# Two-layer network on one core: where the first layer's sums, statistics and comparisons stand in VectorE's queue

## The chip, the cores and the metric

The kernel runs on one core of one Trainium2 chip. A core has five engines with queues of their own: TensorE (PE; its weight loads are listed as PEld), VectorE (DVE), ScalarE (ACT), GpSimd (POOL) and SyncE (SP), which here only issues DMAs. Each engine works through its own queue in the order in which the program was written, and semaphores make one engine wait for another. The metric is the time of one execution in device microseconds, a median over runs.

## What is computed

A batch of 8 sequences of 512 tokens with 512 features goes through two layers. The first is a graph attention, the second a self-attention with conditioned normalization. Cut to what matters:

```
# layer 0: graph attention over the first 20 tokens, for d = 0, 1 (labels, labels transposed)
row_zero  = v.sum(-1) == 0
q_exp     = where(row_zero[..., None], 0, q[:, None, :])
self_feat = concat([v, q_exp], -1) @ W_self.T + b_self
kv        = self_feat[:, :20]
qh, kh    = self_feat @ Wq.T + bq,  kv @ Wk.T + bk          # 16 heads of 32
A         = labels[:, :, :20, :]                            # 11 labels an edge, 0 or 1
mask      = A.sum(-1) > 0
aff       = where(mask, qh.kh / sqrt(32), -9e15) + (A @ w_bias + b_bias)
out_d     = (softmax(aff) @ kv) @ Wout + bout
x         = v + relu(self_feat + out_0 + out_1)
# layer 1
h   = norm(x) * gamma(cond) + beta(cond)
att = softmax(q k^T) v / sqrt(512),  q, k, v from h
h1  = att @ Wp.T + bp + x
out = norm(h1) * gamma(cond) + beta(cond) + h1
```

All of it is fp32.

## The kernel before

**Stages.** A prologue (to about 77 us) prepares weights and the keys of the first layer. Then come 32 *slots* of the first layer (to about 391 us), one for each batch b = 0 to 7 and block c = 0 to 3 of 128 tokens, numbered n = 4b + c. The second layer follows, 128 steps in an order of its own, and is not touched.

**The order is written by hand.** The slots run under a manual schedule: each engine gets its instructions in the order in which the loop at L627 calls the helpers, so a line that moves in the loop moves in the queue of every engine that it uses.

**A slot's scores** pass through five engines, three slots long. In slot n, `scores0` (L525) makes the scores of slot n + 2: TensorE multiplies into a pair of PSUM banks (L532), VectorE adds a row and brings them to SBUF (L536), GpSimd multiplies by the mask (L538). `add_edges` (L541) adds the label bias on GpSimd (L542). `less_top` (L545) takes the maxima on VectorE (L549) and subtracts them on GpSimd (L550). In slot n + 1, `normalize0` (L552) takes exponentials on ScalarE (L553), sums and reciprocals on VectorE (L556, L557), and multiplies on GpSimd (L558). In slot n + 2, `turn_weights` turns the weights on TensorE (L564) and ScalarE copies them out (L566); `result0` (L569) multiplies them with the values (`po`, L574, L576), VectorE adds to the input (L577), and SP stores the block.

**The edges' masks and biases** are made two blocks ahead by `edges` (L248) on VectorE: half 0 sums the 11 labels (L258) and compares with zero (L259), half 1 multiplies by the weights (L262), sums (L263) and adds the constant (L264). For the last block of a batch `far_away` (L266) folds the mask into the bias (L269, L270).

**self_feat of a later batch** comes out of seven quarter products (L347; numbers 1, 2 at c = 2, 6, 7 at c = 3, 4, 5 at c = 0, 3 at c = 1), with sums of weights and of turned tokens made beforehand (`turned_sums` on GpSimd, L345). Each product goes from PSUM into a quarter of `SF` (L373). Three sums of products (`Y0`: product 1, 1 + 6, 1 + 6 + 7) go into four quarters; these adds are gathered in `TO_ADD0` and made at the slot's end (L698 to L700): one at c = 2, three at c = 3.

**Live tokens** are those whose features do not sum to zero. `live_sums` (L289) makes four copies with an accumulated sum on ScalarE (L293) and a comparison on VectorE (L295); `live_of` (L297) turns the result to a row on TensorE (L301) and copies it (L303), for use at c = 2 (L366). For batch b + 2 the sums stand at the end of c = 0 and the row in c = 1 ahead of `result0`.

**The second layer's start** lies in the last slots: statistics of the first finished batch (`norm_stats`, L93, L95, L96 on VectorE, a power on GpSimd, L97) at n = 15 to 18, and its normalization (`norm`, L111 on VectorE) at n = 22 and 23, two blocks each.

Most PSUM banks come from a ring of four (`bank`), score and weight pairs from a ring of two (`pair`).

Of the kernel before, what the change touches and what calls it, by code (L numbers as in the profile page):

```python
# [9 lines left out]
F32 = mybir.dt.float32  # L10
# [3 lines left out]
ALU = mybir.AluOpType  # L14
# [4 lines left out]
B, N, F = 8, 512, 512  # L19
P = 128  # L20
# [5 lines left out]
D2 = 2 * NG  # L26
HM = H * D2
KB = HM // P
L = 11
# [15 lines left out]
def graph_then_self_attention(ctx: ExitStack, tc: tile.TileContext, x, x_t, near, near_t, labels, w_self_t, wq, wk_t,  # L45
                              wout_t, wg_t, wb_t, wqkv_t, wp_t, cols, gate_vecs, rows, out):
    nc = tc.nc
# [13 lines left out]
    edge_bc = vec[:, nv + C * DH:]  # L61
# [28 lines left out]
    def statistics(src, name):  # L90

        st = small.tile([P, 6], F32, tag="st", name=f"st_{name}")
        nc.vector.bn_stats(st, src)  # L93
        mv = small.tile([P, 2], F32, tag="mv", name=f"mv_{name}")
        nc.vector.bn_aggr(mv, st)  # L95
        nc.vector.tensor_scalar(mv[:, 1:2], mv[:, 1:2], EPS, None, ALU.add)  # L96
        nc.gpsimd.tensor_tensor(mv[:, 1:2], mv[:, 1:2], minus_half[:, 0:1], ALU.pow)  # L97
        STATS[name] = mv
# [5 lines left out]
    def norm_stats(b, c, src=None):  # L104
        statistics((src or XQ[b])[:, c, :], f"{b}_{c}")
# [68 lines left out]
    with ExitStack() as l0:  # L174
# [3 lines left out]
        pro = l0.enter_context(tc.tile_pool(name="pro", bufs=1))  # L178
# [36 lines left out]
        def load_vt(b):  # L215
            VT[b] = turned.tile([P, C, N], F32, tag="turned", name=f"vt_{b}")
            for cut in (slice(0, 2), slice(2, C)) if b == 0 else (slice(0, C),):
                nc.sync.dma_start(VT[b][:, cut], blocks(x_t[b])[:, cut])
# [20 lines left out]
            nc.vector.memset(head[DH * j:DH * (j + 1), j:j + 1], 1.0)  # L239

        MASK, ADD, LABELS = {}, {}, {}

        def load_labels(b, halves=(0, 1)):
            for i in halves:
# [3 lines left out]
        def edges(b, c, halves=(0, 1)):  # L248


            if c == 0 and 0 in halves:
                MASK[b] = two.tile([P, C, D2], F32, tag="mask", name=f"mask_{b}")
                ADD[b] = two.tile([P, C, D2], F32, tag="add", name=f"add_{b}")
            src = LABELS[b, c // 2][:, c % 2, :].rearrange("p (m l) -> p m l", l=L)
            weighted = src.bitcast(F32)
            total = two.tile([P, D2], F32, tag="total", name=f"total_{b}_{c}_{halves[0]}")
            if 0 in halves:
                nc.vector.tensor_reduce(total, src, AX.X, ALU.add)  # L258
                nc.vector.tensor_scalar(MASK[b][:, c, :], total, 0.0, None, ALU.is_gt)  # L259
            if 1 not in halves:  # L260
                return
            nc.vector.tensor_tensor(weighted, src, edge_bc[:, None, 0:L].to_broadcast([P, D2, L]), ALU.mult)  # L262
            nc.vector.tensor_reduce(total, weighted, AX.X, ALU.add)  # L263
            nc.vector.tensor_scalar(ADD[b][:, c, :], total, edge_bc[:, L:L + 1], None, ALU.add)  # L264

        def far_away(b):  # L266

# [21 lines left out]
        def live_sums(b):  # L289

            sums = two.tile([P, C], F32, tag="sums", name=f"sums_{b}")
            for c in range(C):
                nc.scalar.activation(X[b][:, c, :], X[b][:, c, :], AF.Copy, accum_out=sums[:, c:c + 1])  # L293
            LT[b] = two.tile([P, C], F32, tag="lt", name=f"lt_{b}")
            nc.vector.tensor_scalar(LT[b], sums, 0.0, None, ALU.not_equal)  # L295

        def live_of(b):  # L297

            pl = bank(f"pl_{b}") if b else pair("pl_0")[:, 0, :]
            for c in range(C):  # L300
                nc.tensor.transpose(pl[:, c * P:(c + 1) * P], LT[b][:, c:c + 1].to_broadcast([P, P]), ident)  # L301
            LIVE[b] = two.tile([P, N], F32, tag="live", name=f"live_{b}")
            nc.scalar.copy(LIVE[b], pl)  # L303
# [25 lines left out]
        SA, TB, Y0, TO_ADD0 = {}, {}, {}, []  # L329
# [100 lines left out]
        for c in range(C):  # L430
            edges(0, c)
# [109 lines left out]
        def add_edges(b, c, engine=nc.gpsimd):  # L541
            engine.tensor_tensor(T[b, c], T[b, c], ADD[b][:, c, None].to_broadcast([P, H, D2]), ALU.add)  # L542
# [26 lines left out]
        def result0(b, c):  # L569
            cut = slice(c * P, (c + 1) * P)  # L570
            po = bank(f"po_{b}_{c}")

            for g in range(HG):
                nc.tensor.matmul(po[:, g * P:(g + 1) * P], SF[b][:, g, cut], ident, is_transpose=True, start=(g == 0), stop=False)  # L574
            for i in range(KB):
                nc.tensor.matmul(po[:, 96 * i:96 * i + P], WT[b, c][:, i, :], vo[:, b % 2, i, :], start=False, stop=(i == KB - 1))  # L576
            nc.vector.scalar_tensor_tensor(X[b][:, c, :], po, 0.0, X[b][:, c, :], ALU.max, ALU.add)  # L577
            nc.sync.dma_start(mid[b, c * P:(c + 1) * P, :], X[b][:, c, :])
# [48 lines left out]
        for n, (b, c) in enumerate(slots):  # L627
            turn_weights(b, c)

            if n + 3 == len(slots):  # L630
                scores0(*slots[n + 2])
            if n + 1 < len(slots):
                normalize0(*slots[n + 1])
            if n + 3 < len(slots):
                scores0(*slots[n + 2])
            if n + 2 < len(slots):
                add_edges(*slots[n + 2], nc.vector if n + 3 == len(slots) else nc.gpsimd)
            if n < 2:
                self_feat(1, (c + 2,))
            elif b + 1 + c // 2 < B:  # L640
                for i in ((4, 5), (3,), (1, 2), (6, 7))[c]:
                    self_feat_product(b + 1 + c // 2, i)
            if 26 <= n < len(slots) - 2:
                less_top(*slots[n + 2])
            if c == 1 and b + 2 < B:
                live_of(b + 2)
                if b + 3 < B:
                    load_vt(b + 3)
            if n in (10, 11, 12, 13):
                keys(1, n - 10, 0)  # L650
            if n in (24, 25):
                for f in (2 * (n - 24), 2 * (n - 24) + 1):
                    turn(0, f)
            group = {26: lambda: q_or_k(0, 0), 27: lambda: q_or_k(1, 0), 29: lambda: value(0), 30: lambda: value(1),
                     31: lambda: value(2)}.get(n, lambda: None)()
            if group:
                group.half(0)
                if n < 30:
                    group.half(1)
            if n == 10:  # L660
                gate_columns(gb)
            result0(b, c)
            if n >= 30:
                group.half(1)
            if b + 1 + c // 2 < B:
                edges(b + 1 + c // 2, (c + 2) % 4, (0,))
            if n < 26:
                less_top(*slots[n + 2])
            if n in (10, 11, 12, 13):
                keys(1, n - 10, 1)  # L670
            if b + 1 + c // 2 < B:
                edges(b + 1 + c // 2, (c + 2) % 4, (1,))
            if c == 0 and b + 2 < B:
                live_sums(b + 2)
            if c == 1:
                if b + 1 < B:
                    far_away(b + 1)
                    load_vo(b + 1)
                if b + 2 < B:
                    load_labels(b + 2, (1,))  # L680
            if c == 0 and b + 2 < B:
                load_labels(b + 2, (0,))
            if c == 2 and b + 2 < B:
                q_row(b + 2)
            if c == C - 1 and b + 3 < B:
                load_x(b + 3)
            if n == 4:
                WG = [weight("wg", wg_t), weight("wb", wb_t)]
            if n == 8:
                gb = gate_vectors()  # L690
                WQ.update({(d, 1): weight(f"wq{d}_1", wq[d]) for d in range(2)})

            if n < 2:
                for i in ((0, 1), (3, 2))[n]:
                    weight_sums0(i)
            if b + 2 + c // 3 < B:
                turned_sums(b + 2 + c // 3, (0, 1, 3, 2)[c])
            for sf, y in TO_ADD0:  # L698
                nc.vector.tensor_tensor(sf, y, sf, ALU.add)
            TO_ADD0.clear()  # L700

            if n in (17, 18, 19, 24):
                i = min(n - 17, 3)
                W1.append(weight(f"w1_{i}", (*(wqkv_t[i] for i in range(3)), wp_t)[i]))
            if n in (23, 28):
                fetch((n - 23) // 5)
            if n == 9:
                early = weight("early", mid[0])
            if 15 <= n < 19:
                norm_stats(0, n - 15, early)  # L710
            for i in {22: (0, 1), 23: (2, 3)}.get(n, ()):
                norm(0, i, early)


# [332 lines left out]
    with tc.manual_schedule():  # L1047
# [22 lines left out]
        for n, (b, g, c) in enumerate(steps):  # L1070
# [28 lines left out]
            early = n % 2 == 0 or each  # L1099
# [12 lines left out]
            if at in OUTPUT_SUMS_AT:  # L1112
                back, i = OUTPUT_SUMS_AT[at]
# [94 lines left out]
```

## Time and profile before

| | us |
|---|---|
| median of 3 runs | 1317.75 (1315.42 to 1318.74) |
| the profiled execution | 1315.49 |
| its span, first to last instruction | 1313.7 |
| granted TensorE clock in it | 0.999 |

The profile is one execution on the chip. Busy time is counted by engine; idle time before an instruction is given with the instruction or semaphore that ended it (its releaser). A line such as L556 is a line of the kernel. A group written "out<-in" tells which tile is written and which are read. Rows that matter for the change, with count, busy time and the mean of one, all on VectorE unless said otherwise:

| line | what | count | busy us | mean ns |
|---|---|---|---|---|
| L259 | mask, 128x40 | 32 | 19.3 | 604 |
| L264 | constant of the bias, 128x40 | 32 | 14.5 | 453 |
| L699 | gathered adds, 128x512 | 24 | 19.7 | 857 |
| L549 | maxima, 128x640 to 128x32 | 32 | 26.2 | 819 |
| L556 | sums of exponentials | 32 | 26.0 | 813 |
| L293 | sums of live tokens (ScalarE) | 32 | 19.8 | 623 |
| L345 | sums of turned tokens (GpSimd), the 12 plain ones | 12 | 19.0 | 1585 |
| L558 | normalized weights (GpSimd) | 32 | 40.7 | 1273 |

### The profile page before, as it was taken

Reading aid. Unit: us, or ns where it says so; the run is one execution under the profiler, and the core shown is the slowest. Engines: PE = TensorE matmul, PEld = TensorE weight load, DVE = VectorE, ACT = ScalarE, POOL = GpSimd, SP = SyncE. Lnnn points to the kernel's source line nnn. Section 1 sums busy time; section 2 is a strip of 40 time slices with the busy share of each in tenths; the row PEclk is TensorE's granted clock in tenths of the full one; section 3 lists DMA queues with packets and bytes.
Section 4 is the critical chain, followed back from the end, with each engine's and each line's share of the span. In section 5 each row is a group of like instructions: output and inputs, shape, how many; then the busy total and the mean of one; then the engine's idle time right before and its main releaser. Section 6 shows DMA issues by size and latency. Waiting matters only on the chain.

```text
span 1313.7 us, 29713 instructions
## 1 busy us (share of the span) xinstructions
PE 1295.4 (99%) x11347; PEld 988.2 (75%) x11347; DVE 974.7 (74%) x1775; ACT 710.1 (54%) x1740; POOL 842.1 (64%) x905
## 2 busy tenths in 40 slices
PE   9999999999999999999999999999999999999997
PEld 6568887777765687777777777777777777777775
DVE  4479887888746678587677859767775976776886
ACT  2333233223225566766666676675666666666664
POOL 0067775677653546677578667747856775775776
PEclk9999999999999999999999999999999999999999
DMA  9533553253221000001002000100200010010010
GB/s 344 180 108 115 179 194 104 96 180 95 92 80 57 1 1 2 2 17 66 1 1 81 1 2 17 66 2 2 81 2 1 18 66 1 2 50 1 10 42 33
DMA packets 46491, 78.65 MB, mean 60 GB/s; under 512 B 9680, under 2 KB 14224, under 8 KB 46352
## 3 DMA queue, kind: packets, MB, share of 16 engines
q1 hardware_dynamic: 45920, 76.22, 17.0%
q8 instruction: 91, 1.49, 0.5%
q10 hardware_dynamic: 432, 0.55, 0.1%
q14 instruction: 48, 0.39, 0.1%
HBM read 59.27 MB, written 17.49 MB: 58 GB/s over the span
## 4 chain that ended last, share of the span: by engine, by line
PE 87%; DVE 8%; POOL 2%; issue 1%; ACT 1%; DMA 0%; POOLq 0%; DVEq 0%; ACTq 0%
PE pst L793 19%; PE pt L949 17%; PE s L924 10%; PE pss L532 8%; PE pao L964 8%; PE psp L836 6%; PE psf_p L359 4%; PE psf L312 2%; PE po L576 2%; PE pqk L138 2%; DVE top L931 2%; PE pz L124 1%; PE ptw L564 1%; PE pw L501 1%; PE pq L482 1%
## 5 line engine op out<-in xcount | busy, mean ns | idle before, releaser
L944 POOL TENSOR_SCALAR e<-e,den 128x512 f32<-128x512 f32 x511 | 366.8, 718 | 262.4 <-DVE den L941 168.5
L936 ACT ACTIVATE e<-s,top 128x512 f32<-128x512 f32 x512 | 348.9, 699 | 131.4 <-DVE top L931 131.2
L931 DVE TENSOR_REDUCE top<-s 128x2 f32<-128x1024 f32 x256 | 301.2, 1218 | 18.5 <-PE s L924 17.1
L949 PEld LDWEIGHTS pt<-ident,e 128*128 128x128 f32 x2048 | 234.5, 141 | 82.5 <-POOL e L944 25.9
L949 PE MATMUL pt<-ident,e 128*128 128x128 f32 x2048 | 289.7, 276 | 3.4 <-ACT et L951 1.3
L951 ACT COPY et<-pt 128x512 f32<-128x512 f32 x369 | 209.6, 597 | 101.1 <-PE pt L949 100.5
L924 PE MATMUL s<-k_pair,q_pair 32*128 32x512 f32 x992 | 143.8, 640 | 0.0
L532 PE MATMUL pss<-kq,sf 128*128 128x320 f32 x512 | 142.9, 432 | 0.0
L964 PEld LDWEIGHTS pao<-et,v 128*32 128x32 f32 x4096 | 107.5, 110 | 44.4 <-issue 44.4
L964 PE MATMUL pao<-et,v 128*32 128x128 f32 x4096 | 126.5, 274 | 0.0
L532 PEld LDWEIGHTS pss<-kq,sf 128*128 128x128 f32 x512 | 94.9, 190 | 36.1 <-ACT kq L489 0.3
L936 ACT ACTIVATION_READ_ACCUMULATOR e<-s,top 128x1 f32 x512 | 109.4, 214 | 0.0
L951 DVE COPY et<-pt 128x512 f32<-128x512 f32 x143 | 96.4, 674 | 3.4 <-PE pt L949 2.8
L538 POOL TENSOR_TENSOR t<-t,mask 128x640 f32<-128x640 f32 x32 | 49.5, 1547 | 65.6 <-DVE t L536 65.6
L558 POOL TENSOR_TENSOR t<-t,den 128x640 f32<-128x640 f32 x32 | 40.7, 1273 | 54.9 <-DVE den L557 54.3
L553 ACT ACTIVATE t<-t 128x640 f32<-128x640 f32 x32 | 23.6, 738 | 91.5 <-POOL t L550 91.5
L550 POOL TENSOR_TENSOR t<-t,top 128x640 f32<-128x640 f32 x32 | 47.4, 1480 | 38.9 <-DVE top L549 38.9
L126 ACT ACTIVATE ht<-pz,gates_t 128x512 f32<-128x512 f32 x32 | 24.7, 778 | 64.2 <-PE pz L124 64.2
L924 PEld LDWEIGHTS s<-k_pair,q_pair 32*128 32x128 f32 x992 | 41.2, 182 | 20.8 <-issue 17.4
L566 ACT COPY wt<-ptw 128x640 f32<-128x640 f32 x32 | 22.2, 694 | 61.2 <-PE ptw L564 61.1
L851 DVE TENSOR_TENSOR xq<-psp,xq 128x512 f32<-128x512 f32 x30 | 20.2, 689 | 45.9 <-PE psp L836 40.7
L793 PE MATMUL pst<-t,w 128*128 128x256 f32 x224 | 53.7, 383 | 0.0
(272 smaller groups left out, 2286.4 us busy)
## 6 DMA issues: line engine op xcount, KB each, us to landing
x<-in_x SPq DMA_DIRECT2D x8, 1024.0 KB
mid<-x SPq DMA_DIRECT2D x32, 256.0 KB
xq<-mid SPq DMA_DIRECT2D x8, 1024.0 KB
out<-o SPq DMA_DIRECT2D x31, 256.0 KB
vt<-in_x_t SPq DMA_DIRECT2D x7, 1024.0 KB
labels<-in_labels SPq DMA_DIRECT2D x16, 440.0 KB
wq<-in_wq SPq DMA_DIRECT2D x4, 1024.0 KB
gate<-gates SPq DMA_DIRECT2D x8, 512.0 KB
```

What stands on the lines that cost most here:

```text
L359: nc.tensor.matmul(o[:, m, :], a[:, k, m * P:(m + 1) * P], t[:, k, :], start=(k == 0), stop=(k == 1))
L532: nc.tensor.matmul(o, SF[b][:, k, cut], KQ[b][:, k, on], start=(k == 0), stop=(k == C - 1))
L538: nc.gpsimd.tensor_tensor(t, t, MASK[b][:, c, None].to_broadcast([P, H, D2]), ALU.mult)
L793: nc.tensor.matmul(out[:, m, :], fixed[:, k, m * P:(m + 1) * P], moving[:, k, :], start=(k == 0), stop=(k == 1))
L836: nc.tensor.matmul(out[:, m, :], t[:, k, m * P:(m + 1) * P], a[:, k, :], start=(k == 0), stop=(k == 1))
L924: nc.tensor.matmul(S[n][j // 2][:, j % 2, :], Q[b, g][on, c * P:(c + 1) * P], K[b, g][on, :], start=True, stop=True)
L931: nc.vector.tensor_reduce(TOP[n][:, 2 * pair:2 * pair + 2], S[n][pair], AX.X, ALU.max, negate=True)
L936: nc.scalar.activation(e, S[n][pair][:, j % 2, :], AF.Exp, bias=TOP[n][:, j:j + 1], accum_out=DEN[n][:, j:j + 1])
L944: engine.tensor_scalar(E[n][j], E[n][j], DEN[n][:, j:j + 1], att_scale, ALU.mult, ALU.mult)
L949: nc.tensor.transpose(pt[:, k * P:(k + 1) * P], E[n][j][:, k * P:(k + 1) * P], ident)
L951: copy(et, pt.rearrange("p (k n) -> p k n", k=C))
L964: nc.tensor.matmul(PAO[b, g][DH * j:DH * (j + 1), at], V[b][:, k, DH * h:DH * (h + 1)], ET[n, j][:, k, :], start=(k == 0), stop=(k == C - 1))
```

## The change

Five things, all in the first layer:

- The gathered adds: instead of all that are on the list, each slot makes one, the oldest. The three of c = 3 are so spread over c = 3, c = 0 and c = 1.
- The statistics of n = 15 to 18 stand between the two halves of `edges`, ahead of the maxima, instead of at the slot's end. Block 0 and 1 of the normalization are made at n = 21 and 22, blocks 2 and 3 at n = 23 as before.
- The sums of live tokens go from the end of c = 0 to c = 1, behind the scores of that slot; the comparison L295 on VectorE goes with them.
- The row of live tokens goes behind `result0` in c = 1, on TensorE and ScalarE.
- The two comparisons and additions with a scalar in `edges` become operations on two tensors, the second one a column repeated along the row; a column of zeros is set once for it.

The count of instructions stays on TensorE, ScalarE, GpSimd and SP, and the order of SP's queue too; VectorE has one memset more.

```diff
         MASK, ADD, LABELS = {}, {}, {}
+        nothing = pro.tile([P, 1], F32, name="nothing")
+        nc.vector.memset(nothing, 0.0)
...
                 nc.vector.tensor_reduce(total, src, AX.X, ALU.add)
-                nc.vector.tensor_scalar(MASK[b][:, c, :], total, 0.0, None, ALU.is_gt)
+                nc.vector.tensor_tensor(MASK[b][:, c, :], total, nothing.to_broadcast([P, D2]), ALU.is_gt)
...
             nc.vector.tensor_reduce(total, weighted, AX.X, ALU.add)
-            nc.vector.tensor_scalar(ADD[b][:, c, :], total, edge_bc[:, L:L + 1], None, ALU.add)
+            nc.vector.tensor_tensor(ADD[b][:, c, :], total, edge_bc[:, L:L + 1].to_broadcast([P, D2]), ALU.add)
...
                 add_edges(*slots[n + 2], nc.vector if n + 3 == len(slots) else nc.gpsimd)
+            if c == 1 and b + 2 < B:
+                live_sums(b + 2)
             if n < 2:
                 self_feat(1, (c + 2,))
...
-            if c == 1 and b + 2 < B:
-                live_of(b + 2)
-                if b + 3 < B:
-                    load_vt(b + 3)
+            if c == 1 and b + 3 < B:
+                load_vt(b + 3)
...
             result0(b, c)
+            if c == 1 and b + 2 < B:
+                live_of(b + 2)
             if n >= 30:
                 group.half(1)
             if b + 1 + c // 2 < B:
                 edges(b + 1 + c // 2, (c + 2) % 4, (0,))
+            if 15 <= n < 19:
+                norm_stats(0, n - 15, early)
             if n < 26:
                 less_top(*slots[n + 2])
             if n in (10, 11, 12, 13):
                 keys(1, n - 10, 1)
             if b + 1 + c // 2 < B:
                 edges(b + 1 + c // 2, (c + 2) % 4, (1,))
-            if c == 0 and b + 2 < B:
-                live_sums(b + 2)
...
-            for sf, y in TO_ADD0:
+            if TO_ADD0:
+                sf, y = TO_ADD0.pop(0)
                 nc.vector.tensor_tensor(sf, y, sf, ALU.add)
-            TO_ADD0.clear()
...
-            if 15 <= n < 19:
-                norm_stats(0, n - 15, early)
-            for i in {22: (0, 1), 23: (2, 3)}.get(n, ()):
+            for i in {21: (0,), 22: (1,), 23: (2, 3)}.get(n, ()):
                 norm(0, i, early)
```

## The prediction

> **What bounds the kernel now.** I read the page's first part, then the busy time by stretch (prologue, the 32 slots of the first layer, the second layer), then what TensorE itself waited for, then the chain and the timeline around those waits. Columns of the stretch: us, then busy time and instructions of PE, PEld, DVE, ACT, POOL, then clock and DMA. Of a wait: total us, times, longest.
>
> ```profile
> PE 1295.4 (99%) x11347; PEld 988.2 (75%) x11347; DVE 974.7 (74%) x1775; ACT 710.1 (54%) x1740; POOL 842.1 (64%) x905
> ...
> 76.60:391.00 314.40, 307.77 (x1816) 243.35 (x1815) 257.72 (x468) 96.95 (x189) 213.74 (x149) 1.00 0.37 122
> ...
> PE ptw L564 <- POOL t L558: 3.5, 7, 1.0
> PE pq L482 <- DVE x L577: 1.6, 4, 0.4
> PE po L574 <- DVE sf L373: 1.4, 1, 1.4
> ```
>
> TensorE is the bound; only where it idles is there time to win. In the slots it idles 314.4 - 307.8 = 6.6 us. The change moves work of VectorE, ScalarE and GpSimd in the slots, and only four transposes a batch on TensorE, so what it can win is small.
>
> A slot starts at its first L564 matmul. Undisturbed slots last 9.86 us (slots 2, 3) and, for c=1, 8.63 (slot 9); slot 24, with two turns of 0.44 more, would last 10.73. Against these the slots lose, idle and refill together: slots 4 to 6: 0.30, 0.44, 0.06; 16 to 19: 0.66, 0.65, 0.81, 0.06; 20 to 22: 1.12, 0.43, 0.06; 23: 0.56; 24: 1.72. Sum 6.9. The L482 waits (slots 10 to 13) are for a PSUM bank that L577 reads out; this edit leaves them.
>
> The timeline at the largest L564 wait (slot 20; start, us, engine, line, then idle and its releaser):
>
> ```profile
> 293.14 2.96 DVE L699 TENSOR_TENSOR sf<-ys,sf 128x512 f32<-128x512 f32 x3
> 293.14 1.80 POOL L345 TENSOR_TENSOR ts<-vt 128x512 f32<-128x512 f32 x1
> 293.21 0.74 ACT L553 ACTIVATE t<-t 128x640 f32<-128x640 f32 x1 [4.01 <-POOL t L550]
> 296.02 0.81 DVE L556 TENSOR_REDUCE den<-t 128x32 f32<-128x640 f32 x1
> ...
> 297.36 1.27 POOL L558 TENSOR_TENSOR t<-t,den 128x640 f32<-128x640 f32 x1 [2.41 <-DVE den L557]
> ...
> 298.69 0.77 PE L564 MATMUL ptw<-ident,t 128*128 128x128 f32 x5 [0.95 <-POOL t L558]
> ```
>
> The exponentials are there at 293.95, but L556 starts at 296.02: three adds stand before it. The second took 1.75 us where 0.68 is usual: it waits for L345 to end on GpSimd. The same triple stands ahead of slots 4, 16 and 24.
>
> **One add a slot.** The 24 adds stay; two of each triple move to the ends of the next two slots. Slot 20: one add issues in 0.60, and L556 follows the exponentials, 2.05 earlier; these also come some 0.6 sooner (293.35), since slot 18's statistics (below) fall into 1.6 us in which L549 waited for L542, and VectorE enters slot 19 in time. L558 then ends near 296.0, and TensorE wants it at 287.71 + 9.86 = 297.57: the stall goes (-1.12). What is late next is L577, which must now wait for `po` (297.8; it was 299.66). L558's earlier end also starts L538 and L542 earlier (L542 to 299.4), so the maxima end at 300.3 and the exponentials for slot 22 at 302.7, against 305.04. The add moved to this slot stands ahead of L556, where the trace has 0.69 us of idle time waiting for the exponentials; it costs nothing. Slot 21's loss (0.43) goes. In slot 21 L542 ends 2.25 earlier (308.57, was 310.82), the slot itself 1.55. The third add follows L270, which waits for L345 anyway, and with one L111 (below) puts 0.60 + 0.54 ahead of L556: L558 ends 316.2, where TensorE wants it at 316.06. 0.1 is lost, and 0.6 more if that earliness is not there. Slots 20 to 22: **-1.5**.
>
> Slots 4 to 6, likewise: L556 moves from 123.93 to 121.90, L577 is back at `po` (126.5, was 127.58), **-0.8**. Slots 23 and 24: L111's first (1.49 us in slot 22, waiting for L345) stays, its second (0.54) goes to slot 21, where GpSimd should be idle: slot 23 -0.3. In slot 24 L574 waits 1.44 for L373, which reads out the bank that `po` takes. VectorE comes to slot 24 earlier by what TensorE gains before it, and two adds less put L373 another 1.20 ahead; with less idle time to refill after, 1.3 of the 1.72 goes. Together **-1.6**.
>
> **Statistics ahead of the maxima** (slots 15 to 18). L93, L95, L96 issue in 0.60 + 0.22 + 0.18 = 1.0 us and now stand before L549 instead of before L556. Where VectorE is late the total is the same; where L556 waits for exponentials, 1.0 is put into the chain L549, L550 (1.58), L553 (0.74). The power on GpSimd (L97, 0.55) goes ahead of L550, but beneath L549 (0.82). Slot 15 pays out of its two removed adds: L556 at 253.1 instead of 255.17, slot 16's 0.66 goes. In slot 16 L549 begins at 259.87 (was 260.95), exponentials end at 263.1. In slot 17 the statistics follow a mask that waits for L542 until 269.0; L549 at 269.9 (was 270.22), and the third add ahead of L556 leaves L558 ending 277.0 (was 277.74): slot 18 keeps its stall. Slots 16 to 19: **-0.7**.
>
> **Comparisons.** Every L259 and L264 stays one instruction. Uncontended rows: 184 and 245 ns. The nearest tensor_tensor is L270, 128x160 in 326 ns; 120 fewer elements at 1/0.96 ns give 201 (the clock from "VectorE: DVE Perf Modes" of the Trainium skill, an estimate). So +17 and -44 ns. The bounds are wide, though: the same L259 takes 0.18 us or 1.3.
>
> ```profile
> 87.88 0.18 DVE L259 TENSOR_SCALAR mask<-total 128x40 f32<-128x40 f32 x1
> ...
> 101.37 1.28 DVE L270 TENSOR_TENSOR add<-add,far 128x160 f32<-128x160 f32 x1
> ...
> 289.14 1.54 POOL L542 TENSOR_TENSOR t<-t,add 128x640 f32<-128x640 f32 x1
> 289.41 1.30 DVE L259 TENSOR_SCALAR mask<-total 128x40 f32<-128x40 f32 x1
> 290.71 0.82 DVE L549 TENSOR_REDUCE top<-t 128x32 f32<-128x640 f32 x1
> ```
>
> The held L259 ends 35 ns after L542: it waits for GpSimd. If a tensor_tensor didn't, all 32 masks would give back 19.3 - 32 x 0.184 = 13.4 us and the 32 sums 14.5 - 7.8 = 6.7. But L270, a tensor_tensor of two SBUF operands, waits too (1.28 for 0.33). The Trainium skill ("SBUF — State Buffer", Who interferes with whom) speaks against this edit in the same way: a Vector instruction with two SBUF inputs contends with a GpSimd instruction that reads SBUF. By row and rule the waits stay: 0. No row has an operand repeated along its innermost dimension, as `nothing` is; that is the open point. And even unheld, L549 reads what L542 writes and would wait just as long; only the statistics of slots 16 to 18 could use the hole, at most 0.9 each, -1.2 of the stalls left. I take **0**, bounds 0 and -1.2; the 32 masks' +17 ns hide in those same waits. The added memset lies under the prologue's DMA waits.
>
> **Sums and row of live tokens.** The four activations and readouts (L293, 2.54 us) go from the end of c=0 to behind the exponentials of c=1; L295 goes behind L536, L301 behind `po`, L303 behind it on ScalarE. The queue of SP keeps its order (vt's load issues as before). ScalarE has room: 2.3 to 3 of 9 us in slots 5, 17, 21. New waits: VectorE's L295 for the sums, with L373 and L577 queued behind it, and TensorE's L301 for L295, with the next L564 queued behind. TensorE comes to L301 8.63 - 0.44 = 8.19 after a slot's start; L295 is ready 2.54 + 0.2 after the exponentials. So it is free if these end by 5.4. In the trace they end at 4.8 (slot 1), 4.6 (9), 6.35 (5), 6.36 (17), 6.35 (21); with the adds gone I get 4.8 for slot 5 (131.15 - 126.3), 5.1 for 21 (302.7 - 297.57), 5.9 for 17 (263.1 - 257.18): 0.6 lost in slot 17, counted in its -0.7. In slot 13 L301 fills the 0.4 wait for L577, but L303 then holds a bank for L482: 0.
>
> **Sum**: 0.8 + 0.7 + 1.5 + 1.6 = 4.6 of the 6.9. The profiled execution took 1315.49 (span 1313.7 and 1.8 around it): 1310.9. The median shown is 1317.75, 2.3 above it; the same 4.6 off gives **1313.1**.
>
> **Rivals.**
> 1. A repeated operand leaves GpSimd alone. For it: no row tests it. Against: rule and L270. Then -4.6 - 1.2 = -5.8: about 1312.0, to 1310.9 if all 6.9 goes.
> 2. The lateness moves instead of going. An add put at the end of c=0 meets L345, and if GpSimd starts first costs 1.75, not 0.68 (in the trace VectorE started first in each slot where one add stood there); the third add has no cover to spare. With 1.1 in three of these slots, 3.3 of the gain goes back: -1.3, near 1316.5. For it: GpSimd is 64% busy and every hold is passed on.
> 3. Slower: the row of live tokens. If the exponentials end at 6.35 in c=1 as slots 5, 17 and 21 show now, L301 is ready at 9.3 where TensorE comes at 8.19: 1.1 each, and 0.7 more where L577 goes late. Over the six batches 6 x 1.8 = 10.8 against 4.6: +6, 1324; with three of them +0.8. It decides once exponentials end later than 5.4 in most c=1 slots. Against: what made them late is what moves away.
> 4. The adds are not what delays TensorE: nothing changes. Against: the timeline above has them between the exponentials and L556. Part of case 2.
>
> **Chances.** Forecast 0.50 (1312 to 1314.5 by itself), rival 1 0.12, rival 2 with 4 0.26, rival 3 0.12. A change under 0.3% (4.0 us) can't be told from none here. Of the forecast 0.42 lies beyond 4.0: faster 0.54. Same: 0.08 + 0.26 + 0.02 = 0.36. Slower 0.10. The range runs from rival 1's end, less the spread of the runs (1.3 us), 1310, to rival 2's end, 1318; 0.10 of rival 3 lies above.
>
> **What would show it.** L699 without an instance of 1.75; L556 of slots 4, 16, 20 within 0.1 of the exponentials; "PE ptw <- POOL t" down from 3.5 to about 1; slot 24's L574 wait from 1.4 to 0.4; the mask still at up to 1.5 us. A TensorE wait for `lt` over 1 us in all would speak for rival 3; masks that never exceed 0.25, for rival 1. PE waiting as much as before, behind other names, would make the forecast wrong.

## The result, and the profile after

| | before | after |
|---|---|---|
| median, us | 1316.90 (1315.12 to 1318.74, 8 runs) | 1321.64 (1319.49 to 1323.32, 8 runs) |
| the profiled execution | 1315.49 | 1323.19 |
| in it, from slot 0's first turn to slot 31's | 314.4 | 319.75 |

The ratio is 1.0037, 95% interval 1.0028 to 1.0047: slower, by 4.7 us in the medians and 5.3 us in the profiled slots. The forecast was 4.6 us the other way. Line numbers in the slots are two higher than before (L266 is the constant, L297 the comparison of the live tokens, L303 their row, L347 the turned sums, L560 the normalized weights, L566 the turns), and the gathered add is L704.

The page's first part of the kernel after (busy time, share of the span, instructions):

```profile
PE 1299.9 (98%) x11347; PEld 991.9 (75%) x11347; DVE 990.6 (75%) x1776; ACT 709.5 (54%) x1740; POOL 836.6 (63%) x905
```

The slots of the kernel after by stretch, from the first L566 of slot 0 to that of slot 31 (columns as before):

```profile
78.99:398.74 319.75, 310.33 (x1816) 245.14 (x1815) 273.71 (x468) 96.59 (x189) 208.12 (x149) 0.99 0.36 119
```

VectorE is busy for 16 us more with the same 468 instructions, and GpSimd for 5.6 us less with the same 149. No work has moved between them: part of both numbers is waiting that counts as busy. GpSimd's sums (L347) hardly wait any more, and VectorE's instructions wait longer; the gathered adds alone have 9.2 of the 16 us. TensorE's waits in the kernel after (us in all, times, longest):

```profile
PE pl L303 <- DVE lt L297: 6.2, 4, 2.3
...
PE ptw L566 <- POOL t L560: 1.3, 4, 0.5
...
PE pq L484 <- DVE x L579: 1.2, 3, 0.4
...
PE po L576 <- DVE sf L375: 0.3, 1, 0.3
```

The wait for GpSimd's weights fell from 3.5 to 1.3 and the one for `sf` from 1.4 to 0.3, as forecast. A wait of 6.2 us for the live tokens' comparison took their place. It looks like the third rival, the row at its new place. The timeline of one of its three large instances (the largest, 2.28 us, is in slot 17), end of slot 4 and slot 5 of the kernel after (start, us, engine, line, then idle and its releaser):

```profile
133.72 1.57 POOL L552 TENSOR_TENSOR t<-t,top 128x640 f32<-128x640 f32 x1 [0.93 <-DVE top L551]
...
134.85 0.50 DVE L266 TENSOR_TENSOR add<-total,vec 128x40 f32<-128x40 f32 x1
135.26 1.27 POOL L347 TENSOR_TENSOR vt<-vt 128x512 f32<-128x512 f32 x1
135.28 1.81 DVE L704 TENSOR_TENSOR sf<-ys,sf 128x512 f32<-128x512 f32 x1
135.33 0.74 ACT L555 ACTIVATE t<-t 128x640 f32<-128x640 f32 x1 [4.06 <-POOL t L552]
...
137.00 0.81 DVE L558 TENSOR_REDUCE den<-t 128x32 f32<-128x640 f32 x1
...
138.34 1.27 POOL L560 TENSOR_TENSOR t<-t,den 128x640 f32<-128x640 f32 x1 [1.81 <-DVE den L559]
138.85 0.79 DVE L297 TENSOR_SCALAR lt<-sums 128x4 f32<-128x4 f32 x1
...
139.79 0.62 PE L303 MATMUL pl<-ident,lt 128*128 128x128 f32 x4 [1.72 <-DVE lt L297]
```

Read from below. TensorE stood 1.72 us for L297. L297 took 0.79 where 0.16 is usual, because it met L560 on GpSimd and ended with it (139.61). Both were late because L558 began at 137.00, though the exponentials were there at 136.07: the single add L704 took 1.81. And the add took so long because it waited for GpSimd's L347: L347 shows its own 1.27, L704 its 0.68 and a wait of 1.13. What the two engines contend for here is called the *port* below, and an instruction that waits for it is *held*.

The same place in the kernel before, end of slot 3 (there three adds follow):

```profile
119.52 1.58 POOL L550 TENSOR_TENSOR t<-t,top 128x640 f32<-128x640 f32 x1 [0.93 <-DVE top L549]
...
120.65 0.49 DVE L264 TENSOR_SCALAR add<-total,vec 128x40 f32<-128x40 f32 x1
121.06 2.95 DVE L699 TENSOR_TENSOR sf<-ys,sf 128x512 f32<-128x512 f32 x3
121.06 1.80 POOL L345 TENSOR_TENSOR ts<-vt 128x512 f32<-128x512 f32 x1
```

Here L345 is the one with the long duration: VectorE was first. The starts tell the same, but only to the nanosecond: in the kernel before, an add that meets a sum of GpSimd starts 3 to 6 ns ahead of it, in the kernel after 16 to 19 ns behind it. It holds for every trace in this document. 220 times an add, a `far` (L269) or a comparison of live tokens starts within 0.3 us of such a sum. Where VectorE starts first or in the same nanosecond (142) it has its usual length; where GpSimd does, by 15 ns or more (78), VectorE takes 1.1 us longer. There is no exception.

How often each went first, from the durations of the add (ns, least / median / most), of the kernel before and then of the kernel after:

```profile
L699 DVE TENSOR_TENSOR sf<-ys,sf x24: 676/679/1751, 112.0 to 334.8; 128x512 f32<-128x512 f32 x24
```

```profile
L704 DVE TENSOR_TENSOR sf<-ys,sf x24: 677/1242/1810, 115.4 to 361.9; 128x512 f32<-128x512 f32 x24
```

Four of 24 adds were long before, each the second of a triple, behind an add that went first. 12 are now, all that meet a sum. What stands just before the add in VectorE's queue is the constant, in its two forms, the kernel before first:

```profile
L264 DVE TENSOR_SCALAR add<-total,vec x32: 244/490/497, 28.4 to 353.2; 128x40 f32<-128x40 f32 x32
```

```profile
L266 DVE TENSOR_TENSOR add<-total,vec x32: 200/506/517, 30.8 to 360.9; 128x40 f32<-128x40 f32 x32
```

Alone, the new form is 44 ns shorter, as I had estimated. But nearly all instances are held behind GpSimd's subtraction of the maxima (L552), and released by its end they take 490 ns in the old form and 506 in the new. That gave the **theory**: VectorE and GpSimd stand behind the same instruction; when it ends, GpSimd's next one is ready at once and VectorE's next one when the constant is done, and 16 ns decide which of the two takes the port for its whole length. Rivals were the row of live tokens by itself, and something in the operation on two tensors other than its length.

### The profile page after: what moved, and what is told of

Its sections match the earlier page's. It is cut to its first block, busy times and chain, and to the rows that moved or that the text cites. A ratio compares the mean times of both kernels' runs of the same rounds, so it can differ in the third digit from the quotient of the medians.

```text
span 1321.4 us, 29708 instructions
## 1 busy us (share of the span) xinstructions
PE 1299.9 (98%) x11347; PEld 991.9 (75%) x11347; DVE 990.6 (75%) x1776; ACT 709.5 (54%) x1740; POOL 836.6 (63%) x905
## 4 chain that ended last, share of the span: by engine, by line
PE 80%; DVE 16%; POOL 2%; issue 1%; ACT 1%; DMA 0%; POOLq 0%; DVEq 0%; ACTq 0%
PE pst L795 19%; PE pt L951 17%; PE s L926 10%; PE pao L966 8%; PE psp L838 6%; PE pss L534 5%; PE pqk L138 2%; PE psf L314 2%; PE psf_p L361 2%; DVE sf L704 2%; DVE top L933 2%; PE po L578 1%; PE pz L124 1%; DVE mask L261 1%; PE pw L503 1%
## 5 line engine op out<-in xcount | busy, mean ns | idle before, releaser
L560 POOL TENSOR_TENSOR t<-t,den 128x640 f32<-128x640 f32 x32 | 40.8, 1274 | 67.9 <-DVE den L559 67.9
L552 POOL TENSOR_TENSOR t<-t,top 128x640 f32<-128x640 f32 x32 | 47.4, 1480 | 36.1 <-DVE top L551 36.1
```

The costliest lines, as they stand in the source:

```text
L552: nc.gpsimd.tensor_tensor(tv, tv, top.to_broadcast([P, 2 * H, NG]), ALU.subtract)
```

## The experiments

All are variants of the kernel after unless it says "before". Ratios are to the kernel before, with 95% intervals; the kernel before had medians of 1316.1 to 1317.6 beside them. "Slots" is the time from slot 0's first turn to slot 31's in the profiled execution (before 314.4, after 319.75).

**1. The constant as it was.** Everything else of the change stays, the masks on two tensors too.

```diff
-            nc.vector.tensor_tensor(ADD[b][:, c, :], total, edge_bc[:, L:L + 1].to_broadcast([P, D2]), ALU.add)
+            nc.vector.tensor_scalar(ADD[b][:, c, :], total, edge_bc[:, L:L + 1], None, ALU.add)
```

> The changed kernel with one edit undone: the constant of the bias is added with tensor_scalar again (the comparison stays on two tensors). Theory P (the port): that operation released VectorE 16 ns later, so that GpSimd's L345 sum starts ahead of the gathered add. Then the add is back at 0.68 us (median; 1.24 in the changed kernel), far at 0.23 (1.35), TensorE's wait for lt falls from 6.2 us to under 3, and the time from 1321.6 to about 1317. Theory R (the row of live tokens is late by itself, behind sums that follow the exponentials): the wait for lt stays above 5 and the time above 1320.

1311.89, ratio 0.9966 (0.9954 to 0.9978); slots 309.8, which is 4.6 below before. The gain is about twice the expected one (to 1317). One operation of 128x40 in its old form turns the change from 4.7 us slower to 5.7 faster. The end of slot 4 again, in this run:

```profile
131.72 0.49 DVE L266 TENSOR_SCALAR add<-total,vec 128x40 f32<-128x40 f32 x1
132.12 0.68 DVE L704 TENSOR_TENSOR sf<-ys,sf 128x512 f32<-128x512 f32 x1
132.13 1.81 POOL L347 TENSOR_TENSOR vt<-vt 128x512 f32<-128x512 f32 x1
132.20 0.74 ACT L555 ACTIVATE t<-t 128x640 f32<-128x640 f32 x1 [2.56 <-POOL t L552]
...
132.97 0.82 DVE L558 TENSOR_REDUCE den<-t 128x32 f32<-128x640 f32 x1 [0.17 <-ACT t L555]
```

The long duration is back on L347, the sums of exponentials wait here for nothing but the exponentials, and all 24 adds take 0.68. Of the wait for `lt` one of 0.5 us is left, in slot 17.

**2. The constant alone, on the kernel before.** The same line changed in the other direction, and nothing else.

> The kernel before with one edit alone: the constant of the bias added as an operation on two tensors. Theory P: the first add of each slot goes from 0.68 to 1.80 us and far from 0.23 to 1.35, since GpSimd starts first; the triple's second add falls from 1.75 to 0.68 in exchange, so that only the slots with c = 2 (one add) lose 1.1 each of VectorE's slack: 0 to +1.5 us. Theory R: durations of the adds unchanged, 0.

1324.17, ratio 1.0055 (1.0043 to 1.0068); slots 322.0, +7.5. The direction is as the theory has it; the size was far underestimated. I had priced the adds by themselves; the waits of this run (TensorE's, columns as above) show the whole chain late:

```profile
PE ptw L564 <- POOL t L558: 8.7, 11, 1.3
PE pq L482 <- DVE x L577: 1.6, 4, 0.4
...
PE po L574 <- DVE sf L373: 1.5, 1, 1.5
```

9 adds took 1.80, the comparisons of live tokens that follow the constant at the end of c = 0 took 1.28 instead of 0.16, and `far` (128x160, 0.23) 1.35: whatever VectorE has next there is held, not the add alone. With the row at its old place, the loss stands as a wait for GpSimd's weights.

**3. Sums and row of live tokens at their old places**, the constant on two tensors.

> The changed kernel with sums and row of live tokens at their old places. Theory R: all that was lost comes back, and the adds' gain shows: about 1313. Theory P: TensorE no longer waits for lt, but the adds still take 1.8 us behind GpSimd, so waits of ptw for GpSimd come back (2 to 4 us in all): 1315 to 1318.

1319.66, ratio 1.0026 (1.0016 to 1.0037); slots 318.7. Both theories had expected less. But of the 5.3 us only 1.1 leave with the row, and the name of the wait changes:

```profile
PE ptw L566 <- POOL t L560: 5.6, 9, 0.9
PE pq L484 <- DVE x L579: 1.6, 4, 0.4
...
PE pl L303 <- DVE lt L297: 1.1, 3, 0.7
```

So the 6.2 us that TensorE waited for L297 were not the row's doing. With the row in c = 1 it is what TensorE meets first; without it, TensorE meets the weights, which are just as late.

**4. Adds and statistics only** (before, with the gathered adds one a slot and the statistics and normalization moved), and **5. adds only** (before, with one add a slot).

```diff
-            for sf, y in TO_ADD0:
+            if TO_ADD0:
+                sf, y = TO_ADD0.pop(0)
                 nc.vector.tensor_tensor(sf, y, sf, ALU.add)
-            TO_ADD0.clear()
```

> The changed kernel with both comparisons and the row undone: what is left of the change is the adds, one a slot, and the statistics ahead of the maxima. Both theories: faster than before by 3 to 5 us, 1312 to 1314; adds at 0.68 us in the median, no wait for lt. If it is not faster, the predicted gain of the adds was wrong too.

> The kernel before with one edit alone: one gathered add a slot. The forecast's arithmetic (the triples ahead of slots 4, 16, 20 and 24 go, and with them the waits behind them): faster by 3 to 5 us, near 1313. In slots with c = 0 the comparison of live tokens stands between the constant and the add, so the add there should start behind GpSimd's L345 and take 1.75 us (as 3 of 24 did in the run with adds and statistics); that keeps some of the gain.

Adds and statistics: 1313.48, ratio 0.9971 (0.9961 to 0.9981), slots 311.1 (-3.3). Adds alone: 1313.56, ratio 0.9979 (0.9971 to 0.9987), slots 312.6 (-1.8). In both, three adds at the end of c = 0 take 1.76: there the comparison of live tokens, still at its old place, stands between constant and add, and GpSimd goes first. By these two executions the adds are worth 1.8 us in the slots, and the statistics with the normalization 1.5. The medians do not confirm this split: the intervals overlap. For the adds alone 3 to 5 us had been expected.

**6. Which property of the constant: its kind or its length?** Two runs. In one the operation on two tensors covers 20 of the 40 columns (the sum is made in place; the constant of the transposed labels is left out, so that output differs). In the other the scalar form is kept, and made longer by writing each of the 40 columns twice.

```diff
-            nc.vector.tensor_reduce(total, weighted, AX.X, ALU.add)
-            nc.vector.tensor_tensor(ADD[b][:, c, :], total, edge_bc[:, L:L + 1].to_broadcast([P, D2]), ALU.add)
+            nc.vector.tensor_reduce(ADD[b][:, c, :], weighted, AX.X, ALU.add)
+            nc.vector.tensor_tensor(ADD[b][:, c, 0:NG], ADD[b][:, c, 0:NG], edge_bc[:, L:L + 1].to_broadcast([P, NG]), ALU.add)
```

> The changed kernel, but the sum goes into the bias tile itself and the operation on two tensors adds the constant to 20 of its 40 columns (the constant of the transposed labels is left out). It has the kind of the changed kernel and the length of the old form: 20 columns fewer are 21 ns. Theory T (a race by time: who asks first when L552 lets go): VectorE is first again, adds 0.68 us in the median, 1311 to 1313.5. Theory K (an operation on two tensors hands the port on differently, whatever its length): adds at 1.80, 1320 to 1323.

```diff
-                ADD[b] = two.tile([P, C, D2], F32, tag="add", name=f"add_{b}")
+                TWICE[b] = two.tile([P, C, 2, D2], F32, tag="add", name=f"add_{b}")
+                ADD[b] = TWICE[b][:, :, 0, :]
...
-            nc.vector.tensor_tensor(ADD[b][:, c, :], total, edge_bc[:, L:L + 1].to_broadcast([P, D2]), ALU.add)
+            nc.vector.tensor_scalar(TWICE[b][:, c], total[:, None, :].to_broadcast([P, 2, D2]), edge_bc[:, L:L + 1], None, ALU.add)
```

> The changed kernel with the constant added by tensor_scalar, but on 80 elements a partition (the 40 sums twice, the second copy unused): the old kind, some 20 ns longer than the old form. Theory T: GpSimd is first, adds 1.80 us, 1320 to 1323. Theory K: adds 0.68, 1311 to 1313.5.

Shorter: 1310.72, ratio 0.9958 (0.9945 to 0.997), slots 309.6, all adds 0.68. Longer: 1320.31, ratio 1.0027 (1.0018 to 1.0036), slots 318.8, 12 adds at 1.80. The groups of the two, the shorter operation on two tensors first (busy us, mean ns):

```profile
L704 DVE TENSOR_TENSOR sf<-ys,sf 128x512 f32<-128x512 f32 x24 | 16.3, 679 | 0.0
...
L266 DVE TENSOR_TENSOR add<-add,vec 128x20 f32<-128x20 f32 x32 | 13.7, 428 | 1.1
```

```profile
L705 DVE TENSOR_TENSOR sf<-ys,sf 128x512 f32<-128x512 f32 x24 | 29.8, 1242 | 0.0
...
L267 DVE TENSOR_SCALAR add<-total,vec 128x80 f32<-128x80 f32 x32 | 14.8, 461 | 1.1
```

Held, they take 485 and 507 ns at the median. An operation on two tensors of 485 ns is harmless, a scalar one of 507 is not. The kind is out; between 490 and 506 ns lies the point at which the order turns.

**7. The same race from the other side.** The kernel after, its constant untouched; GpSimd gets one tiny memset ahead of its sums, 0.10 us.

```diff
             if b + 2 + c // 3 < B:
+                nc.gpsimd.memset(pause, 0.0)
                 turned_sums(b + 2 + c // 3, (0, 1, 3, 2)[c])
```

> The kernel after, untouched on VectorE (the constant stays an operation on two tensors, 506 ns when held), with one memset of a 128x1 tile (0.10 us by the profile's row) put on GpSimd ahead of each of its sums L347. Theory T (the port goes to the one that asks first): GpSimd now asks some 0.1 us later than VectorE, so the gathered adds take 0.68 us throughout, far_away 0.23, and the time is that of the run with the constant as a scalar: 1311.9, ratio 0.996 to 0.997, slots about 310. If it is not the order of asking that decides, but something in the operation on two tensors itself, the adds stay at 1.8 us and the time at 1321 to 1322.

1311.03, ratio 0.9959 (0.9946 to 0.9973); slots 309.9. The constant still takes 506 ns, and every add 0.68:

```profile
131.20 0.68 DVE L706 TENSOR_TENSOR sf<-ys,sf 128x512 f32<-128x512 f32 x1
131.22 1.79 POOL L348 TENSOR_TENSOR vt<-vt 128x512 f32<-128x512 f32 x1
```

VectorE's add now starts 20 ns ahead of the sum, and work *added* to GpSimd makes the kernel some 10 us faster than it was without. This settles it: the order in which the two engines ask is the cause, whatever sets it.

**8. The masks in their old form too** (run 1 with L261 as a scalar comparison; no operation on two tensors of the change is left).

> e1 with the mask's comparison in its old form too, so that no operation on two tensors is left. Theory T: the mask, whichever its form, waits for GpSimd's L542 and the maxima behind it wait for the same: 1311.9 as in e1, +-0.7. Against the run without comparisons and row (1313.5) this then gives the new place of the sums and the row: -1.6. If the repeated operand had freed the mask in part, e13 would be slower than e1 by up to 1.2 us: 1313.1.

1310.56, ratio 0.9955 (0.9943 to 0.9968); slots 309.2, 0.6 below run 1. 0.5 of it lies in slot 2, which the runs show at 9.86 or at 10.3 to 10.8 with either form (10.58 in run 4, whose masks are scalar; 9.86 in the last run below, whose masks are not). I put that down to how the prologue ends, which was not tried. The intervals overlap: no effect of the masks can be seen. Against run 4, the new place of sums and row is worth 2.0 us of slots, 1.3 of them without slot 2; the prediction had it at nothing.

**9. A better version.** Run 1 with the sums of live tokens back at the end of c = 0, their comparison behind the reciprocal of c = 1 and the row at its new place; so no comparison stands between constant and add, and TensorE never waits for it. Then the same without the constant: the sum writes the bias directly, and `far_away` adds constant and far in one operation.

```diff
-            nc.vector.tensor_reduce(total, weighted, AX.X, ALU.add)
-            nc.vector.tensor_scalar(ADD[b][:, c, :], total, edge_bc[:, L:L + 1], None, ALU.add)
+            nc.vector.tensor_reduce(ADD[b][:, c, :], weighted, AX.X, ALU.add)
...
-            nc.vector.tensor_tensor(ADD[b], ADD[b], far, ALU.add)
+            nc.vector.scalar_tensor_tensor(ADD[b], ADD[b], edge_bc[:, L:L + 1], far, ALU.add, ALU.add)
```

> The changed kernel with the constant as tensor_scalar, and the sums of live tokens at the end of c = 0 as before, their comparison in c = 1 behind L557's reciprocal, the row behind result0. Against e1 (1311.9) this takes away the wait of slot 17 for the sums (0.48 and refill) and the comparison's wait for L558 (0.63 where it is held): slot 17 from 9.23 to 8.6, slot 18 somewhat shorter: 0.5 to 1.3 us below e1. If the comparison delays L558 or the row, no gain.

> e10 without the 32 instructions of the constant: the sum L265 writes the bias directly, and far_away adds constant and far in one operation of three operands. The constant was what queued behind GpSimd's L552 ahead of the gathered add; now the add itself, or far_away, queues there first. Theory T (who has its request at the port at the end of L552 gets it): the waiting add is served ahead of GpSimd's next sums, so no add takes over 0.7 us plus its wait for L552, and 0.49 us of VectorE goes from each slot; what is left of TensorE's waits in the slots is about 2 us, of which at most 1 goes: 1309.0 to 1310.0, ratio 0.9945 to 0.9955. If taking the constant away lets GpSimd's sums start first (as the slower constant did), adds at 1.8 us come back: over 1313.

1310.04, ratio 0.9952 (0.994 to 0.9965), slots 308.8; without the constant 1309.56, ratio 0.9948 (0.9934 to 0.9961), slots 307.9. Both beat the kernel before and the change; between the two the medians decide nothing. The end of slot 4 without the constant:

```profile
128.36 1.57 POOL L557 TENSOR_TENSOR t<-t,top 128x640 f32<-128x640 f32 x1 [1.14 <-DVE top L556]
...
129.37 1.12 DVE L711 TENSOR_TENSOR sf<-ys,sf 128x512 f32<-128x512 f32 x1
129.90 1.72 POOL L352 TENSOR_TENSOR vt<-vt 128x512 f32<-128x512 f32 x1
```

Now the add itself waits for L557 (0.44 of its 1.12) and has the port when it ends at 129.93. It needs nothing to be quick: it was there before GpSimd asked. In this run TensorE's losses in the slots that the change aimed at are down to two waits, 0.10 and 0.15 us.

## Why the prediction was wrong

**The step that failed** is "Comparisons": "By row and rule the waits stay: 0", with bounds 0 and -1.2. The waits of the constant did stay, and that is why it cost so much. I compared *uncontended* durations ("So +17 and -44 ns"), found the new constant shorter, and took a held instruction as one whose own length no longer matters. It matters for what comes next: released by L552, it takes 16 ns more than before, and GpSimd goes first. The price of the step, from run 1 to the kernel after, is 319.75 - 309.77 = 10.0 us in the slots (9.8 in the medians; about 1 of the 10.0 is a dip of the clock, see the end), at a term for which I let no loss in at all. The bound on the side of a loss should have been open: an instruction at which two engines are released together decides who goes next, and the profile of before showed the margin, L699 and L345 starting at the same hundredth of a microsecond, 3 to 6 ns apart.

**What was passed over.** The Trainium skill ("SBUF — State Buffer", SBUF: two separate sides, and Who interferes with whom) states that the one that starts first has the shared port pair for its whole instruction, and that the order of issue, not the shape, decides who blocks. I used the page for the question whether a mask waits, and not for this sentence. The 220 meetings and runs 6 and 7 agree with it, and the runs give the margin: 490 or 506 ns.

**The rest of the sum** came out in run 1, which has everything but the constant. By groups of slots, from the first turns (before, run 1):

| slots | forecast | run 1 |
|---|---|---|
| 4 to 6 | -0.8 | 29.15 to 28.29: -0.86 |
| 16 to 19 | -0.7 | 40.39 to 39.66: -0.73 |
| 20 to 22 | -1.5 | 29.96 to 28.29: -1.67 |
| 23, 24 | -1.6 | 22.87 to 21.25: -1.62 |

With slot 2 (+0.50) and the rest (-0.26) it makes -4.64 in the slots against the 4.6 forecast, and 1311.89 against 1313.1 as a median. In the kernel after part of these gains came too: slots 4, 16, 20 and 24 went from 10.16, 10.52, 10.98 and 12.45 to 9.94, 9.86, 9.94 and 11.27. (Even held, one add of 1.80 delays L558 less than three that take 2.96: in slot 20 it begins 0.93 after the exponentials, before it was 2.07.) They were lost above all in c = 1, where slots 5, 17 and 21 went from 9.07, 9.28 and 9.06 to 10.53, 11.46 and 10.53; slots 2, 9, 10, 18 and 22 lost 0.4 to 0.7 each.

**The statistics**: slots 16 to 19, forecast at -0.7, gained 0.81 in run 4; with the adds alone (run 5) they lost 0.06. **The split** of the sum was not right, though its total was. Adds and statistics together gave 3.3 of the 4.6 (run 4). The rest came with the move of the sums and the row (run 8), which takes the comparison of live tokens out of c = 0; the prediction had that move at 0 and its gain among the adds.

**The masks**: right. In the kernel after (ns, least / median / most)

```profile
L261 DVE TENSOR_TENSOR mask<-total,nothing x32: 199/706/1423, 29.4 to 358.7; 128x40 f32<-128x40 f32 x32
```

```profile
141.21 1.54 POOL L544 TENSOR_TENSOR t<-t,add 128x640 f32<-128x640 f32 x1
141.38 1.42 DVE L261 TENSOR_TENSOR mask<-total,nothing 128x40 f32<-128x40 f32 x1
```

the operation with a repeated operand is held as the others are (this one ends 0.05 us after GpSimd's L544), and alone it is 15 ns longer than the scalar form (17 were estimated). Rival 1 falls.

**The row of live tokens**: right in run 1, one wait of 0.5 in slot 17 where 0.6 was counted. Its rival 3 described the kernel after well: TensorE waits for `lt`, 1.7 to 2.3 us in three of the c = 1 slots. I had written that such a wait "would speak for rival 3". It spoke for something upstream of it: runs 1 and 3 show that the row alone loses next to nothing and that without it most of the loss stays.

**Rival 2** named the mechanism, an add that meets the sums of turned tokens and costs 1.75 if GpSimd starts first, with a chance of its own, but kept out of the sum with "in the trace VectorE started first". That was true, by a margin which the same change took away; the sign asked for, "L699 without an instance of 1.75", failed 12 times. It was priced for three slots; 12 adds were hit, and with L560 late six of the comparisons met it, where three do in run 1. In five slots `far` was held too (L271, 0.23 to 1.35), but there the hold only moved from the operation behind it (L272, 1.28 to 0.33), at a net cost of 0.19 us.

## What to carry to other kernels

Where two engines share a port and stand behind the same instruction, look at who goes next and by how much: read it from the durations (the one with its usual length was first) and, to the nanosecond, from the starts, and treat every edit of the instruction just before as one that can turn the order, even one that makes it shorter when alone. A duration taken from an instance that was not held did not tell here what the same instruction takes when it is. And the wait that ends last at the bound engine names the place where lateness surfaces; before blaming what stands there, put it back where it was and see whether the loss goes or only changes its name.

## What was not expected of the hardware

The two forms of the constant rank one way alone (245 and 200 ns) and the other way held (490 and 506). That 16 ns are worth 10 us of a 1320 us kernel was the surprise, and that 0.1 us of useless GpSimd work buys them back.

In the profiled execution of the kernel after, TensorE's clock fell. Stretches of slot 17 and 18 (columns as before, clock third from the end):

```profile
263.05:274.50 11.45, 9.17 (x49) 7.49 (x48) 11.24 (x20) 3.88 (x10) 8.25 (x7) 0.96 0.46 155
274.50:285.57 11.07, 11.07 (x52) 9.08 (x52) 10.12 (x18) 5.09 (x8) 7.34 (x7) 0.89 0.27 75
```

Slot 18 has no idle time, and yet took 11.07 us: the records give a clock of 0.5 from 273.54 to 276.95 us, beginning in the last 0.1 us of the 2.28 us for which TensorE waited. The run with the longer scalar form has the same wait of 2.27 us in slot 17 and no such dip, and its slots 17 to 19 took 31.79 against 32.75: about 1 us for the dip. Of the 8 runs of the kernel after 3 have a mean clock of 0.997 instead of 0.999; whether for the same reason isn't known, as only one of them has a trace. It looks as if a stall of this size can cost a second time, though not always. In each trace the changes of the clock lie a whole multiple of 3.413 us apart. On that grid 2.20 of the 2.28 us fall into one step, the one at whose end the clock falls; in the run with the longer scalar form a step's end splits the wait into 1.38 and 0.89. That may be what decides; two executions do not show it.
